# A four-layer graph attention stack: token blocks moved by DMA and transposed on VectorE in layers 0 and 2, and exp read straight from the score bank

## The chip, the cores and the metric

The kernel runs on one core of a Trainium2 chip. A core has TensorE (PE; its weight loads are shown apart as PEld), VectorE (DVE), ScalarE (ACT), GpSimd (POOL) and SyncE (SP), each with its own queue of instructions that it works through in order. SP issues most of the DMAs. The metric is the device time of the whole program in microseconds, as a median over runs.

## The reference, cut to what matters

The input `x` has 128 graphs of 64 nodes with 512 features, `adj` says which nodes are joined. Four layers follow each other, all in fp32:

```python
for layer in 0, 1, 2, 3:
    h = relu(layernorm(x))            # per node, over 512 features
    x = x + attention_layer(h, adj)

# layers 0 and 2: 4 heads of 64
q, k, v = h @ Wq, h @ Wk, h @ Wv      # 512 -> 256 each
s = where(adj, q k^T / 8, -max)
out = softmax(s) v @ Wo + bo
# layer 1: 8 heads, a second layernorm with gamma and beta ahead of q, k, v
# layer 3: 8 heads, a map, cosine neighbours, a softmax, a graph convolution, relu
```

The nodes of all graphs make 8192 rows ("tokens"). TensorE contracts over partitions, so the projections need `h` with features on partitions, `hT`, while the layernorm works with tokens on partitions. Something has to transpose every layer's normalised tokens.

## The kernel before, in words

The 8192 tokens are worked in 16 steps of 512 per layer; `(l, s)` names step `s` of layer `l`. A step's tokens are one tile `xin` of 128 partitions by 4 blocks of 512 features. Two such tiles exist. One step goes through these stages, each written as a Python generator:

- `loads` (line 470) brings `xin` in by two DMAs on SP, from the input or from the layer before, which was stored in DRAM.
- `layernorms` (496) takes the statistics on VectorE, the power of -1/2 on POOL, and normalises on ScalarE, in place in `xin`.
- `transposes` (554) makes `hT` (two buffers). In layers 0 and 2, and in the first two steps of layers 1 and 3, TensorE transposes 16 blocks of 128x128 into PSUM banks `ptr`, four to a group (570), and ScalarE copies each group of four into `hT` (574). In steps 2 to 15 of layers 1 and 3 `turned_tokens` (510) does it without TensorE: ScalarE and POOL copy sixteen 32x512 pieces of `xin` into a buffer `t` so that the 32x32 blocks stand in their places (534, 531), and VectorE's transpose, which turns each 32x32 block in itself, finishes (544).
- `sums_of_b` (356) makes on POOL the four differences that a seven-product (Winograd) scheme needs, in a buffer `t` (three exist).
- `projections` (729) runs the products, all at line 613 in PSUM banks `mA`, `mB` and `mC`. Results come out by ScalarE copies (630, 650) and VectorE adds (643, 654).
- `front` (1158) makes the scores (930) into `sc`, and `softmax_parts` (934) masks them on VectorE (941), takes the row maximum (947), subtracts it into an SBUF tile `E` (949), which gives the score bank back, and takes exp on ScalarE (952). Row sums (959), a reciprocal (963) and a product on POOL (965) follow. The bank `sc` is a single one, and the products of attention and values, `po` (1097), use the same.
- `turns` and `transposed` (967) transpose the attention with ScalarE copies (974) and VectorE (979). `attention` (1075) forms `po`, the output projection (613 again) and its adds to the residual `xres`, on POOL (1024, 1045) and VectorE (643). `store` (1058) writes the result by SP (1065). `residuals` (1009) loads `xres` by SP (1020), `masks` (983) loads `adj` (988).

The order of instructions on each engine is not written out by hand. A small planner, `Order` (93), takes the generators with priorities. Each `yield` names an engine and an assumed duration, such as `act(0.6)`; a wait is a `yield` of an event. The planner runs the generators against each other on these assumed durations and emits the instructions in the order that results. On the chip each engine follows that order, with semaphores for the data. Buffers come from rings: `Ring.new` (165) waits in the plan for the buffer's last user. The ring `qk` (three buffers of 128x2048 fp32) holds the projected queries and keys.

Of the kernel before, what the change touches and what calls it, by code (L numbers as in the profile page):

```python
# [10 lines left out]
AF = mybir.ActivationFunctionType  # L11
ALU = mybir.AluOpType
AX = mybir.AxisListType

P = 128
D = 512
N = 64
TB = 4
NC = D // P
# [184 lines left out]
def pe(us):  # L204
    return ("pe", us, 0.25)
# [6 lines left out]
def dve(us):  # L212
    return ("dve", us, 0.1)


def act(us):
    return ("act", us, 0.1)
# [11 lines left out]
def gnn_stack(ctx: ExitStack, tc: tile.TileContext, a: dict, out: bass.AP):  # L229
    nc = tc.nc  # L230
    x_d = a["x"]
    NG = x_d.shape[0] // (P * TB)
    od = Order()

    def ring(tag, n, shape, dtype=F32, space=None):
        kw = {} if space is None else {"space": space}
        p = ctx.enter_context(tc.tile_pool(name=tag, bufs=n, **kw))
        return Ring(od, p, n, shape, dtype, tag)
# [12 lines left out]
    r_h = ring("h", 2, [P, NC, TB * P])  # L251
    r_t = bank("t", 3, [P, NC, 2, H])
    r_qk = ring("qk", 3, [P, NC, TB * P])
# [15 lines left out]
    x_done = {}  # L269
# [86 lines left out]
    def sums_of_b(B, T, vector=False):  # L356

        n = T.shape[2]
        for o, i0, i1 in ((T[:, 0], B(0, 1), B(0, 0)), (T[:, 1], B(1, 1), T[:, 0]),
                          (T[:, 2], B(1, 1), B(0, 1)), (T[:, 3], B(1, 0), T[:, 1])):  # L360
            if vector:
                yield dve(0.9)
                nc.vector.tensor_tensor(o, i0, i1, ALU.subtract)  # L363
            else:
                yield pool(1.42)
                nc.gpsimd.tensor_tensor(o, i0, i1, ALU.subtract)  # L366
# [70 lines left out]
    def scales(v):  # L437

        mv = small.tile([P, 2, 2], F32, tag="mv", name="mv")
        for t in range(2):  # L440
            st = small.tile([P, 6], F32, tag="st", name="st")
            yield dve(0.68)
            nc.vector.bn_stats(st, v[:, t, :])  # L443
            yield dve(0.17)
            nc.vector.bn_aggr(mv[:, t, :], st)
        rs = small.tile([P, 3, 2], F32, tag="rs", name="rs")
        yield dve(0.25)
        nc.vector.tensor_scalar_add(rs[:, 1, :], mv[:, :, 1], LN_EPS)  # L448
        yield pool(0.75)
        nc.gpsimd.tensor_tensor(rs[:, 0, :], rs[:, 1, :], mhalf[:, :2], ALU.pow)  # L450
        yield dve(0.45)
        nc.vector.scalar_tensor_tensor(rs[:, 2, :], mv[:, :, 0], -1.0, rs[:, 0, :],  # L452
                                       ALU.mult, ALU.mult)
        return rs

    def normalize(v, rs, func):
        for t in range(2):
            yield act(0.81)
            nc.scalar.activation(v[:, t, :], v[:, t, :], func, bias=rs[:, 2, t:t + 1],  # L459
                                 scale=rs[:, 0, t:t + 1])  # L460

    hT, hB, h_ready, h_done, t_done = {}, {}, {}, {}, {}

    def quarters(v):

        return lambda j, k: v[:, 2 * j:2 * j + 2, k * H:(k + 1) * H]

    loaded, l_ready = {}, {}

    def loads(steps):  # L470
        for l, s in steps:
# [22 lines left out]
    normed, n_ready = {}, {}  # L494

    def layernorms(steps, half):

        for l, s in steps:
            yield l_ready[l, s, half]
            whole, xe = loaded.pop((l, s, half))  # L500
            x = whole[:, 2 * half:2 * half + 2, :]
            rs = yield from scales(x)
            yield from normalize(x, rs, AF.Relu)
            if l == 1:
                rs = yield from scales(x)
                yield from normalize(x, rs, AF.Identity)
            normed[l, s] = whole, xe
            n_ready[l, s, half].set()

    def turned_tokens(l, s):  # L510
# [40 lines left out]
        h_ready[l, s].set()  # L551
        return h

    def transposes(steps):

        for l, s in steps:
            if (l, s) in [(1, 2), (1, 3), (1, 4), (1, 5), (1, 6), (1, 7), (1, 8), (1, 9), (1, 10), (1, 11), (1, 12), (1, 13), (1, 14), (1, 15), (3, 2), (3, 3), (3, 4), (3, 5), (3, 6), (3, 7), (3, 8), (3, 9), (3, 10), (3, 11), (3, 12), (3, 13), (3, 14), (3, 15)]:
                h = yield from turned_tokens(l, s)
            else:
                h, h_done[l, s] = yield from r_h.new("hT")  # L560
                hT[l, s] = h
            for half in range(0 if (l, s) in [(1, 2), (1, 3), (1, 4), (1, 5), (1, 6), (1, 7), (1, 8), (1, 9), (1, 10), (1, 11), (1, 12), (1, 13), (1, 14), (1, 15), (3, 2), (3, 3), (3, 4), (3, 5), (3, 6), (3, 7), (3, 8), (3, 9), (3, 10), (3, 11), (3, 12), (3, 13), (3, 14), (3, 15)] else 2):
                yield n_ready[l, s, half]
                x, xe = normed[l, s]
                for t in range(2):
                    b = 2 * half + t
                    pt, pe_ = yield from r_tr.new("ptr")
                    for c in range(NC):
                        yield pe(0.115)
                        nc.tensor.transpose(pt[:, c, :], x[:, b, c * P:(c + 1) * P], ident)  # L570
                    if b == TB - 1:
                        xe.set()
                    yield act(0.6)
                    nc.scalar.copy(h[:, :, b * P:(b + 1) * P], pt)
                    pe_.set()
                if (l, s, half) == (0, 0, 0):
                    yield from has_h(l, s, h)
            if (l, s) != (0, 0) and (l, s) not in [(1, 2), (1, 3), (1, 4), (1, 5), (1, 6), (1, 7), (1, 8), (1, 9), (1, 10), (1, 11), (1, 12), (1, 13), (1, 14), (1, 15), (3, 2), (3, 3), (3, 4), (3, 5), (3, 6), (3, 7), (3, 8), (3, 9), (3, 10), (3, 11), (3, 12), (3, 13), (3, 14), (3, 15)]:
                yield from has_h(l, s, h)
            yield from sums_of_b(quarters(h), hB[l, s][1], (l, s) == (0, 0))  # L580
            hB[l, s][2].set()
            if (l, s) == (0, 0):
                first_t.set()

    def has_h(l, s, h):
        T, t_done[l, s] = yield from r_t.new("T")
        hB[l, s] = (quarters(h), T, od.event())
        h_ready[l, s].set()
# [138 lines left out]
    st, p_ready, s_ready, p_used, o_used, turn = {}, {}, {}, {}, [], []  # L727
# [203 lines left out]
                                         lT[r, c, k], rT[r, c, k], start=True, stop=True)  # L931
        return S, e

    def softmax_parts(S, se, E, mask, neg, masked):

        m = mask.rearrange("p b k -> p (b k)")
        n = m.shape[1]
        sv = S.rearrange("p a (c m) -> p (a c) m", m=n)
        shape = [P, 1024 // n, n]
        yield dve(1.5)  # L940
        nc.vector.copy_predicated(sv, m[:, None, :].to_broadcast(shape),
                                  negs[:, neg:neg + 1, None].to_broadcast(shape))
        masked.set()
        S3 = S.rearrange("p a (i k) -> p (a i) k", k=N)
        mx = soft.tile([P, 16], F32, tag="mx", name="mx")
        yield dve(1.2)
        nc.vector.tensor_reduce(mx, S3, AX.X, ALU.max)
        yield dve(1.2)
        nc.vector.tensor_tensor(E, S3, mx[:, :, None].to_broadcast([P, 16, N]), ALU.subtract)  # L949
        se.set()  # L950
        yield act(1.06)
        nc.scalar.activation(E, E, AF.Exp, scale=0.125)  # L952
        sm = soft.tile([P, 2, 16], F32, tag="sm", name="sm")
        yield from row_sums(sm[:, 0, :], E)
        return sm

    def row_sums(o, E):
        yield dve(1.2)
        nc.vector.tensor_reduce(o, E, AX.X, ALU.add)  # L959
# [230 lines left out]

    def softmax(l, z, u, S, se, m, masked):
        E = z["e", u][0]
        sm = yield from softmax_parts(S, se, E, m, (0, 1, 0, 2)[l], masked)
        z["sm", u] = sm
        if l < 3:
            yield from divide(E, sm[:, 0, :])
            z["e_ready", u].set()
        z["exp", u].set()
# [73 lines left out]

    steps = [(l, s) for l in range(4) for s in range(NG)]
    for k in steps:
        for e in (p_ready, s_ready, p_used, h_ready, x_done):
            e[k] = od.event()
        for half in range(2):
            l_ready[(*k, half)], n_ready[(*k, half)] = od.event(), od.event()
    with tc.manual_schedule():
        od.spawn(weights(), 4)  # L1280
        od.spawn(loads(steps), 4)
        for half in range(2):
            od.spawn(layernorms(steps, half), 4)
        od.spawn(transposes(steps), 3)
        od.spawn(projections([k for k in steps if k[0] < 3]), 5)
        od.spawn(fronts(steps), 1)
        od.spawn(turns(steps), 1)
        od.spawn(attentions(steps), 2)
        od.run()
# [45 lines left out]
```

## Time and profile before

| What | Value |
|---|---|
| Median of 3 runs | 2790.13 us (2788.91 to 2795.86) |
| Profiled execution, its own time | 2791.22 us |
| Its span, first to last instruction | 2789.2 us |
| Mean granted TensorE clock | 0.993 |
| Busy share PE, PEld, DVE, ACT, POOL | 98%, 85%, 68%, 67%, 58% |
| TensorE transposes `ptr` (line 570) | 576 records |
| DMA | 238.51 MB in 160430 packets |

A page row gives the line, engine, operation, output and inputs, shapes and count, then the busy time in us and the mean ns of one, and last the idle time of that engine just before, with what ended it. A fp32 product appears as two records of line 613, a transpose as one. In the chain of waits the columns are who waited, for whom, the total in us, how often, and the longest. "SPq" is SP's queue of DMA issues.

### The profile page before, as it was taken

To read this page: it belongs to the slowest core of one execution; us is meant where nothing else is said; L and a number is where in the kernel's file an instruction comes from. 1 tells how busy PE (TensorE), PEld (TensorE's weight loads), DVE (VectorE), ACT (ScalarE), POOL (GpSimd) and SP (SyncE) were. 2 spreads that over 40 slices of the span, in tenths; PEclk is the share of its full clock that TensorE was granted. 3 is DMA by queue.
4 is the path that set the end of the run, shared out by engine and by line. 5 is a ranking of instruction groups with operands and counts; after the bars stand their busy time and mean duration, and the time that the engine had idled before them with its cause. 6 is when DMAs were issued, how large, how long until landed. Compare 5 with 4: busy or idle time off the path is not lost.

```text
span 2789.2 us, 63654 instructions
## 1 busy us (share of the span) xinstructions
PE 2723.9 (98%) x26728; PEld 2362.1 (85%) x26728; DVE 1896.2 (68%) x2780; ACT 1872.4 (67%) x3149; POOL 1608.2 (58%) x1242
## 2 busy tenths in 40 slices
PE   8999999999999999999999999999999999999997
PEld 7888888888888888888888888878888888888876
DVE  6766767677767667766657666746777667776656
ACT  5756756688777777776656656657566776677644
POOL 5667667645435445446656576676665656555543
PEclk9999999999999999999999999999999999999998
DMA  4333333212112111112322242332422233223221
GB/s 157 108 107 109 108 116 114 96 63 77 47 62 77 47 61 64 61 47 97 122 93 92 93 138 93 108 104 78 111 64 63 71 93 86 64 63 84 73 63 47
DMA packets 160430, 238.51 MB, mean 86 GB/s; under 512 B 23952, under 2 KB 69008, under 8 KB 160144
## 3 DMA queue, kind: packets, MB, share of 16 engines
q1 hardware_dynamic: 145632, 219.98, 25.4%
q10 hardware_dynamic: 14512, 14.47, 1.6%
q8 instruction: 210, 3.44, 0.5%
q14 instruction: 76, 0.62, 0.1%
HBM read 166.77 MB, written 67.63 MB: 84 GB/s over the span
## 4 chain that ended last, share of the span: by engine, by line
PE 91%; DVE 4%; POOL 2%; ACT 1%; issue 1%; DMA 1%; POOLq 0%; SPq 0%; ACTq 0%; DVEq 0%
PE mA L613 46%; PE mC L613 23%; PE mB L613 12%; PE sc L930 5%; PE po L1097 2%; PE ptr L570 2%; PE po L1242 1%; PE mmn L872 1%; POOL xres L1045 1%; POOL xres L1024 1%; ACT F L974 1%; DVE xres L643 1%; DVE E L949 0%; DVE t L363 0%; POOL E L965 0%
## 5 line engine op out<-in xcount | busy, mean ns | idle before, releaser
L974 ACT COPY F<-E 32x512 f32<-32x512 f32 x768 | 472.5, 615 | 41.0 <-POOL E L965 26.3
L1045 POOL TENSOR_TENSOR xres<-xres,u 128x512 f32<-128x512 f32 x192 | 259.9, 1361 | 296.3 <-ACT u L1040 236.1
L1024 POOL TENSOR_TENSOR xres<-xres,u 128x512 f32<-128x512 f32 x192 | 260.8, 1380 | 23.0 <-DMA xres<-x 17.0
L366 POOL TENSOR_TENSOR t<-hT 128x512 f32<-128x512 f32 x126 | 181.4, 1440 | 145.7 <-DVE hT L544 89.0
L459 ACT ACTIVATE xin<-xin,rs 128x512 f32<-128x512 f32 x320 | 247.8, 810 | 19.4 <-DVE rs L452 15.6
L630 ACT COPY v<-mA 128x256 f32<-128x256 f32 (+1 forms) x192 | 92.0, 479 | 218.5 <-PE mA L613 205.5
L534 ACT COPY t<-xin 32x512 f32<-32x512 f32 x364 | 224.1, 616 | 6.4
L450 POOL TENSOR_TENSOR rs<-rs,mhalf 128x2 f32<-128x2 f32 x160 | 115.9, 726 | 192.0 <-DVE rs L448 168.7
L443 DVE BATCH_NORM_STATS2 st<-xin 128x6 f32<-128x512 f32 x320 | 214.9, 672 | 15.8 <-DMA xin<-in_x 7.7
L613 PE MATMUL mA<-w_vo,t 128*128 128x128 f32 (+1 forms) x1152 | 204.5, 312 | 1.1 <-ACT u L1040 1.1
L613 PE MATMUL mA<-t,w_qk 128*128 128x256 f32 x768 | 185.9, 381 | 1.5 <-DVE t L363 1.5
L965 POOL TENSOR_TENSOR E<-E,sm 128x1024 f32<-128x1024 f32 x64 | 127.8, 1997 | 100.6 <-DVE sm L963 87.3
L613 PE MATMUL mA<-t,w_q 128*128 128x256 f32 x744 | 179.2, 383 | 0.0
L613 PEld LDWEIGHTS mA<-w_vo,t 128*128 128x128 f32 x1152 | 166.2, 191 | 14.6 <-ACT u L1040 4.3
L613 PE MATMUL mA<-t,w_k 128*128 128x256 f32 x744 | 177.3, 381 | 0.0
L366 POOL TENSOR_TENSOR t<-hT,t 128x512 f32<-128x512 f32 x126 | 168.3, 1336 | 7.7 <-DVE hT L544 4.2
L959 DVE TENSOR_REDUCE sm<-E 128x16 f32<-128x1024 f32 x128 | 154.9, 1210 | 12.8 <-ACT E L952 12.1
L613 PEld LDWEIGHTS mA<-t,w_qk 128*128 128x128 f32 x768 | 144.4, 192 | 20.3 <-DVE t L363 1.7
L613 PEld LDWEIGHTS mA<-t,w_q 128*128 128x128 f32 x744 | 140.5, 191 | 20.8 <-issue 1.2
L613 PEld LDWEIGHTS mA<-t,w_k 128*128 128x128 f32 x744 | 140.3, 190 | 19.4
L979 DVE STREAM_TRANSPOSE pt<-F 128x1024 f32<-128x1024 f32 x96 | 118.7, 1236 | 49.8 <-ACT F L974 49.6
L1040 ACT COPY u<-mA 128x512 f32<-128x512 f32 x144 | 84.4, 586 | 97.7 <-PE mA L613 88.8
(217 smaller groups left out, 6908.9 us busy)
## 6 DMA issues: line engine op xcount, KB each, us to landing
x<-xres SPq DMA_DIRECT2D x96, 512.0 KB
xin<-x SPq DMA_DIRECT2D x96, 512.0 KB
xres<-x SPq DMA_DIRECT2D x64, 512.0 KB
xres<-in_x SPq DMA_DIRECT2D x32, 512.0 KB
u<-rs SPq DMA_DIRECT2D x128, 128.0 KB
xres<-x SPq DMA_DIRECT2D x64, 256.0 KB
out<-xres SPq DMA_DIRECT2D x64, 256.0 KB
xin<-in_x SPq DMA_DIRECT2D x30, 512.0 KB
```

Source lines behind the costliest of these rows:

```text
L366: nc.gpsimd.tensor_tensor(o, i0, i1, ALU.subtract)
L443: nc.vector.bn_stats(st, v[:, t, :])
L459: nc.scalar.activation(v[:, t, :], v[:, t, :], func, bias=rs[:, 2, t:t + 1], scale=rs[:, 0, t:t + 1])
L534: nc.scalar.copy(o, v)
L613: nc.tensor.matmul(o, l, r, start=(first and m == 0 and k == 0), stop=(k == KC - 1), skip_group_check=True)
L930: nc.tensor.matmul(S[g * N:(g + 1) * N, par, col], lT[r, c, k], rT[r, c, k], start=True, stop=True)
L959: nc.vector.tensor_reduce(o, E, AX.X, ALU.add)
L965: nc.gpsimd.tensor_mul(E, E, sm[:, :, None].to_broadcast([P, 16, N]))
L974: nc.scalar.copy(F[g * N + 32 * k:g * N + 32 * (k + 1), :, 32 * i:32 * (i + 1)], E[g * N + 32 * i:g * N + 32 * (i + 1), :, 32 * k:32 * (k ...
L979: nc.vector.transpose(o, F)
L1024: nc.gpsimd.tensor_add(xr[:, t, :], xr[:, t, :], bo[l])
L1045: nc.gpsimd.tensor_add(v, v, both(u))
```

## The change

In steps 2 to 15 of layers 0 and 2 the tokens are no longer transposed on TensorE. A new stream `moves` issues sixteen DMAs on SP for each step, from SBUF to SBUF. Each takes 32 partitions of the normalised `xin` and writes, in pieces of 32 numbers, 32 partitions of a buffer `F` from the ring `qk`, so that the 32x32 blocks stand in their places. `by_vector` then turns the blocks with two VectorE transposes into `hT`. TensorE's transposes and ScalarE's copies out of `ptr` go away for these 28 steps. `xin` is given back when the DMAs have read it, and a step's moves wait, in the plan, until the `F` before has been turned.

In all steps of layers 0 and 2 the softmax no longer subtracts the maximum on VectorE. It multiplies the maximum by -1/8, and ScalarE takes exp from the score bank in sixteen instructions of 64 columns, each with its own row maximum as bias, into `E`. The score bank is given back after the last of them.

```diff
+    def moves(steps):
+        fe = None
+        for l, s in steps:
+            for half in range(2):
+                yield n_ready[l, s, half]
+            if fe:
+                yield fe
+            x, xe = normed.pop((l, s))
+            F, fe = yield from r_qk.new("F")
+            Fv = F.rearrange("p c n -> p (c n)").rearrange("p (a i f) -> p a i f", i=4, f=32)
+            xv = x.rearrange("p b (c k f) -> p (b c) k f", c=NC, k=4)
+            for k in range(4):
+                for i in range(4):
+                    yield ("sp", 0.7, 4.0)
+                    nc.sync.dma_start(Fv[32 * k:32 * (k + 1), :, i], xv[32 * i:32 * (i + 1), :, k])
+            xe.set()
+            before, fe = fe, od.event()
+            moved[l, s] = F, before, fe
+            f_ready[l, s].set()
+
+    def by_vector(l, s):
+        yield f_ready[l, s]
+        F, fe, taken = moved.pop((l, s))
+        h, h_done[l, s] = yield from r_h.new("hT")
+        hT[l, s] = h
+        F = F.rearrange("p c n -> p (c n)").rearrange("p (b c n) -> p b c n", b=TB, c=NC)
+        for b in range(0, TB, 2):
+            yield dve(1.25)
+            nc.vector.transpose(h.rearrange("p c (b n) -> p b c n", b=TB)[:, b:b + 2], F[:, b:b + 2])
+        fe.set()
+        taken.set()
+        return h
...
     def transposes(steps):
         for l, s in steps:
-            if (l, s) in [(1, 2), ... (3, 15)]:
+            if (l, s) in by_dma:                      # steps 2 to 15 of layers 0 and 2
+                h = yield from by_vector(l, s)
+            elif (l, s) in turned:                    # steps 2 to 15 of layers 1 and 3
                 h = yield from turned_tokens(l, s)
...
-        yield dve(1.2)
-        nc.vector.tensor_tensor(E, S3, mx[:, :, None].to_broadcast([P, 16, N]), ALU.subtract)
-        se.set()
-        yield act(1.06)
-        nc.scalar.activation(E, E, AF.Exp, scale=0.125)
+        if narrow:                                    # layers 0 and 2
+            yield dve(0.1)
+            nc.vector.tensor_scalar(mx, mx, -0.125, None, ALU.mult)
+            for i in range(16):
+                yield act(0.21)
+                nc.scalar.activation(E[:, i, :], S3[:, i, :], AF.Exp, bias=mx[:, i:i + 1], scale=0.125)
+            se.set()
+        else:
+            yield dve(1.2)
+            nc.vector.tensor_tensor(E, S3, mx[:, :, None].to_broadcast([P, 16, N]), ALU.subtract)
+            se.set()
+            yield act(1.06)
+            nc.scalar.activation(E, E, AF.Exp, scale=0.125)
...
+        od.spawn(moves(by_dma), 3)
         od.spawn(transposes(steps), 3)
```

More of the change, by code (lines that the diff above doesn't have):

```diff
@@ L466, in quarters @@
         return lambda j, k: v[:, 2 * j:2 * j + 2, k * H:(k + 1) * H]
-    loaded, l_ready = {}, {}
+    loaded, l_ready, moved, f_ready = {}, {}, {}, {}
+    by_dma = [(0, 2), (0, 3), (0, 4), (0, 5), (0, 6), (0, 7), (0, 8), (0, 9), (0, 10), (0, 11), (0, 12), (0, 13), (0, 14), (0, 15), (2, 2), (2, 3), (2, 4), (2, 5), (2, 6), (2, 7), (2, 8), (2, 9), (2, 10), (2, 11), (2, 12), (2, 13), (2, 14), (2, 15)]
+    turned = [(1, 2), (1, 3), (1, 4), (1, 5), (1, 6), (1, 7), (1, 8), (1, 9), (1, 10), (1, 11), (1, 12), (1, 13), (1, 14), (1, 15), (3, 2), (3, 3), (3, 4), (3, 5), (3, 6), (3, 7), (3, 8), (3, 9), (3, 10), (3, 11), (3, 12), (3, 13), (3, 14), (3, 15)]
     def loads(steps):
@@ L552, in turned_tokens @@
         return h
+    def moves(steps):
[29 more added lines that the diff above has]
+        return h
     def transposes(steps):
         for l, s in steps:
-            if (l, s) in [(1, 2), (1, 3), (1, 4), (1, 5), (1, 6), (1, 7), (1, 8), (1, 9), (1, 10), (1, 11), (1, 12), (1, 13), (1, 14), (1, 15), (3, 2), (3, 3), (3, 4), (3, 5), (3, 6), (3, 7), (3, 8), (3, 9), (3, 10), (3, 11), (3, 12), (3, 13), (3, 14), (3, 15)]:
+            if (l, s) in by_dma:
+                h = yield from by_vector(l, s)
+            elif (l, s) in turned:
                 h = yield from turned_tokens(l, s)
@@ L561, in transposes @@
                 hT[l, s] = h
-            for half in range(0 if (l, s) in [(1, 2), (1, 3), (1, 4), (1, 5), (1, 6), (1, 7), (1, 8), (1, 9), (1, 10), (1, 11), (1, 12), (1, 13), (1, 14), (1, 15), (3, 2), (3, 3), (3, 4), (3, 5), (3, 6), (3, 7), (3, 8), (3, 9), (3, 10), (3, 11), (3, 12), (3, 13), (3, 14), (3, 15)] else 2):
+            for half in range(0 if (l, s) in turned + by_dma else 2):
                 yield n_ready[l, s, half]
@@ L577, in transposes @@
                     yield from has_h(l, s, h)
-            if (l, s) != (0, 0) and (l, s) not in [(1, 2), (1, 3), (1, 4), (1, 5), (1, 6), (1, 7), (1, 8), (1, 9), (1, 10), (1, 11), (1, 12), (1, 13), (1, 14), (1, 15), (3, 2), (3, 3), (3, 4), (3, 5), (3, 6), (3, 7), (3, 8), (3, 9), (3, 10), (3, 11), (3, 12), (3, 13), (3, 14), (3, 15)]:
+            if (l, s) != (0, 0) and (l, s) not in turned:
                 yield from has_h(l, s, h)
@@ L932, in scores, with softmax_parts @@
         return S, e
-    def softmax_parts(S, se, E, mask, neg, masked):
+    def softmax_parts(S, se, E, mask, neg, masked, narrow=False):
         m = mask.rearrange("p b k -> p (b k)")
@@ L1192, in softmax @@
         E = z["e", u][0]
-        sm = yield from softmax_parts(S, se, E, m, (0, 1, 0, 2)[l], masked)
+        sm = yield from softmax_parts(S, se, E, m, (0, 1, 0, 2)[l], masked, l in (0, 2))
         z["sm", u] = sm
@@ L1274, in gnn_stack @@
     for k in steps:
-        for e in (p_ready, s_ready, p_used, h_ready, x_done):
+        for e in (p_ready, s_ready, p_used, h_ready, f_ready, x_done):
             e[k] = od.event()
```

## The prediction

> **What bounds the kernel now.** I read the page first: busy time by engine, and the chain of work that ended last.
>
> ```profile
> PE 2723.9 (98%) x26728; PEld 2362.1 (85%) x26728; DVE 1896.2 (68%) x2780; ACT 1872.4 (67%) x3149; POOL 1608.2 (58%) x1242
> PE 91%; DVE 4%; POOL 2%; ACT 1%; issue 1%; DMA 1%; POOLq 0%; SPq 0%; ACTq 0%; DVEq 0%
> ```
>
> TensorE is busy for 98% of the span and carries 91% of the chain; nothing else is near. An average hides stages, so I then took busy time by stretches: two inside layers 0 and 2, which the change touches, and one in layer 1. The columns are the stretch, its length, then busy microseconds of PE, weight loads, DVE, ACT and POOL, the granted clock, DMA share and GB/s.
>
> ```profile
> 200.00:340.00 140.00, 138.60 (x1340) 124.25 (x1339) 99.66 (x158) 90.52 (x156) 94.49 (x73) 1.00 0.36 115
> 560.00:900.00 340.00, 339.85 (x3084) 294.06 (x3083) 237.41 (x352) 266.77 (x412) 162.07 (x136) 1.00 0.19 63
> 1560.00:1700.00 140.00, 135.57 (x1356) 120.17 (x1355) 89.52 (x141) 85.35 (x145) 91.33 (x71) 0.99 0.34 115
> ```
>
> Layers 0 and 2 are TensorE-bound too, with a little idle time. Over 60 to 480 us, PE is idle 420 - 410.7 = 9.3 us, over 1420 to 1840 us 13.7 us: 23 us in some 29 steps, 0.8 us a step. A step (one `sc` group to the next, 264.04 to 292.80) lasts 28.8 us. So what leaves TensorE's queue here is gained, unless something else becomes late by more. Next, who makes PE wait in 60 to 480 us (the chain of waits, PE), and what SP's queue waits for:
>
> ```profile
> PE mC L613 <- DVE xres L643: 3.6, 2, 1.8
> PE mB L613 <- DVE xres L643: 2.6, 2, 1.3
> PE po L1097 <- DVE E L949: 2.4, 3, 1.0
> ```
>
> ```profile
> SPq L486 <- PE ptr L570: 201.9, 14, 24.6
> SPq L1065 <- DVE xres L643: 144.6, 15, 29.6
> SPq L1020 <- DMA x<-xres: 37.0, 25, 4.0
> ```
>
> PE's few waits are for residual adds on DVE, and for the score bank that L949 gives back. SP is idle most of the time: its loads stand ready and wait for `xin`, given back by the transposes, and its stores for the last residual add. Input arrives long before its use, which gives a longer way to `hT` room.
>
> **What a transpose group costs.** The timeline, PE's weight loads around one group:
>
> ```profile
> 243.17 0.41 PEld L613 LDWEIGHTS mA<-w_vo,t 128*128 128x128 f32 x2
> ...
> 243.60 0.57 PEld L570 LDWEIGHTS ptr<-ident,xin 128*128 128x128 f32 x4
> ...
> 244.14 0.30 PEld L613 LDWEIGHTS mA<-w_vo,t 128*128 128x128 f32 x2
> ```
>
> From the group's first load to the next product's is 244.14 - 243.60 = 0.54 us, the same at 248.79, 250.52, 257.44 and 272.32. There is no bubble before it: two loads of `mA` take 0.43 us here and elsewhere.
>
> **What the Trainium skill says.** "DMA: Bandwidth & Descriptors", Specifications, says that transfers under 512 B fall below line rate because they are read, modified and written. The trace agrees: its packet records give 97 ns for 2 KB packets (21 B/ns), 12.6 ns for the 4096 of 128 B (10 B/ns), half the rate but far from a fixed cost of a large packet. "ScalarE: Activation LUTs", What ACT_TABLE_LOAD costs, prices an ACTIVATE with a per-partition bias at 280 ns + 0.833 ns an element, neighbours overlapping by 93 ns; L634 (256 elements) took 471 ns where this gives 493, so the trace is a little below it.
>
> **The change, by parts.** Rows used (groups by shape):
>
> ```profile
> L574 ACT COPY hT<-ptr 128x512 f32<-128x512 f32 x144 | 84.4, 588 | 14.7 <-PE ptr L570 13.1 <-issue 1.0
> L949 DVE TENSOR_TENSOR E<-sc,mx 128x1024 f32<-128x1024 f32 x96 | 117.0, 1219 | 1.8
> L952 ACT ACTIVATE E<-E 128x1024 f32<-128x1024 f32 x96 | 101.5, 1057 | 9.4 <-DVE E L949 8.9
> L979 DVE STREAM_TRANSPOSE pt<-F 128x1024 f32<-128x1024 f32 x96 | 118.7, 1236 | 49.8 <-ACT F L974 49.6
> L634 ACT ACTIVATE kT<-mA,vecs 128x256 f32<-128x256 f32 x96 | 40.3, 471 | 27.6 <-PE mA L613 26.7
> ```
>
> *Off TensorE:* 28 steps x 4 groups x 0.54 = 60.5 us. The chain's share of `ptr` (2.0%, 56 us over 576) would give 448 x 0.097 = 43 us, its busy time (90.5 us over 576) 70 us. I take 60: pace in the queue is what TensorE gets back. Nothing is added to TensorE.
>
> *ScalarE, a step:* four copies go, 4 x 0.588 = 2.35, and one exp, 1.06. Sixteen exps of 64 columns come. From L634, one takes 471 - 192 x 0.836 = 310 ns (the slope from copies of 256 and 512 columns, 372 and 586), and follows its neighbour after about 0.21 (pairs of L459, 0.81 each, take 1.52). So +3.5, up to 16 x 0.31 = 5.0. Net +0.05 to +1.6 us. ScalarE stands at 90.5/140, 18.6 us of a step of 28.7; with 18.6 to 20.2 in a step of 26.5, 70 to 76%. Hidden under TensorE.
>
> *VectorE, a step:* L949 goes (1.22), a 128x16 multiply comes (about 0.16, as L448), and two transposes of 1.24. Net +1.4. From 20.4 to 21.8 us in 26.5: 82%. Hidden, but this is the engine whose in-order queue holds the residual adds that PE waits for; without cover it would cost 28 x 1.4 = 39 us. POOL keeps its work, 19.4 us, 73% of the shorter step.
>
> *The score bank:* it is held by the sixteen exps rather than until the subtract. That is +0.16 + 3.5 - 1.22 = +2.4 us, with interleaved copies perhaps 4. There is one bank, which `po` needs. Now the subtract ended at 243.15 and `po` followed at 258.61: 15 us spare. In the built order, in the steady part, some 15 us of products stand between `sc` and `po` again. Cost nothing; without that cover 32 x 2.4 = 77 us.
>
> *SP and DMA, a step:* sixteen moves of 64 KB in 128 B pieces. Present issues take 0.36 to 0.63 us (L1020 to L1154), so 5.8 to 10 us on SP over the 2.9 us there; no present issue has 512 pieces. Below, a move could cost 0.36; above, the 1.4 us each that two of L1020 once took (2.86 at 325.95). I take 0.6. The engines' time is 8192 packets x 12.6 ns / 16 = 6.5 us on 0.36 x 28.7 = 10.3: 63% of a step, no bound.
>
> *Order:* in the built order some twelve moves stand before a step's store and four behind it, and behind these the next loads of `xres` and `xin`. The loads of `xin` wait until the moves land; each move waits for the DMA eight before it. The store waits for the last residual add, with the moves behind it queued on SP. Then `xin` must land before VectorE's statistics, ahead of the next residual adds on its queue. I sum this way from the last add: POOL 1.3, stores 0.7, four moves 2.4, landing 3, `xres` 0.4, `xin` issue 0.5 and landing 4, 12 to 13 us. Both landings are estimates: a store kept SP waiting 37.0/25 = 1.5 us more, while the first load of all, at the start, took 7.1 us in the chain. Statistics stand some two thirds of a step later, about 18 us. Slack 5 us, or 2 with a landing of 7. So it is hidden, but this is the thinnest cover.
>
> *Sum:* -60.5, and I let PE's idle time of 0.8 us a step grow by half as VectorE fills: 28 x 0.4 = +11. Net -49.5. The profiled execution took 2791.2 (span 2789.2), 1 us over the median of 2790.1; from the median, **2740**.
>
> **Rivals.**
>
> *Half is eaten:* VectorE at 82% in program order delays residual adds and bank releases more than I allow: 0.7 to 1.8 us a step, 20 to 52 us, 2750 to 2782, centre 2765. For: PE's present waits are of this kind. Against: in layer 1 VectorE is 70% busy and ScalarE 78%, and PE idles 0.15 us in 340.
>
> *SP sets the step (slower):* if a move holds SP for 1.9 us (piece generation at 512 pieces, or waiting for the DMA eight before it to land), SP needs 16 x 1.9 + 2.9 = 33.3 us, 4.6 over the present step: 28 x 4.6 = +129, near 2920; at 1.75, 2855. It bites from (26.5 - 2.9)/16 = 1.47 us and loses from (28.7 - 2.9)/16 = 1.6. Against: the longest ordinary issue is 0.63.
>
> *The score bank* could replace the wait removed: were the spare of 15 us gone, +77 - 60 gives 2807. Speaks for it only that `po` already waited for L949 three times, at most 1.0 us.
>
> **How the numbers follow.** Gain kept (2724 to 2748): 0.58. Half eaten: 0.25, and with it a remainder near no change, 0.04. SP: 0.10. Bank: 0.03. The range is 2722 to 2784, leaving some 0.16 outside, mostly above; the likeliest case's own range is 2724 to 2748. About 0.3%, 8 us, is what a measurement can tell from no change: faster 0.83, same 0.04, slower 0.13.
>
> **What would show it.** Right: PE's busy time down by about 60 us, `ptr` at 128 records; sixteen exps some 0.2 us apart; moves issued in under 0.8 us; PE idle in layers 0 and 2 about 34 us over those 28 steps. Wrong: PE waits for `hT` or `t` behind F, VectorE waits at its F transposes or statistics for DMA, SP's issues well over 1 us, or `po` waits for the exps.

## The result: 2751.9 us, 39 us faster

| | before | after |
|---|---|---|
| Median | 2791.27 us (2788.91 to 2795.86) | 2751.89 us (2749.39 to 2755.36) |
| Ratio to before, 95% interval | | 0.9855 [0.9839, 0.9871] |
| Profiled execution, its span | 2791.2, 2789.2 us | 2751.8, 2750.0 us |
| Mean granted TensorE clock | 0.993 | 0.991 |

The forecast was 2740 us with a range of 2722 to 2784. Direction and range hold. Of the net 49.5 us that the sum gave, 39 arrived, which is outside the likeliest case's own range (2724 to 2748) and at the edge of "half is eaten".

The busy times by engine and the chain that ended last, after:

```profile
PE 2678.9 (97%) x26280; PEld 2320.6 (84%) x26280; DVE 1956.6 (71%) x2836; ACT 1889.6 (69%) x3517; POOL 1615.5 (59%) x1242
PE 91%; DVE 4%; ACT 2%; DMA 1%; SPq 1%; POOL 1%; issue 1%; POOLq 0%; ACTq 0%; DVEq 0%
```

TensorE is still the bound. Its busy time fell by 45.0 us and its idle time rose from 65.3 to 71.1 us (span less busy): -45.0 + 5.8 = -39.2, the whole difference. The three engines beside it rose by 60, 17 and 7 us, and the chain gives the three together 7%, as before.

SP's moves, by the tile `F` (shortest, median and longest in ns), and two groups by shape:

```profile
L571 SPq DMA_DIRECT2D F<-xin x448: 585/631/2797, 46.1 to 1731.7; - x150
```

```profile
L586 DVE STREAM_TRANSPOSE hT<-F 128x1024 f32<-128x1024 f32 x56 | 67.0, 1223 | 0.7 <-DMA F<-xin 0.6
L992 ACT ACTIVATE E<-sc,mx 128x64 f32<-128x64 f32 x512 | 122.0, 352 | 21.6 <-DVE mx L989 21.3
```

A move holds SP for 0.63 us at the median (0.6 was taken). VectorE waited for a move once, 0.6 us: the moves land in time. A narrow exp takes 352 ns by itself (310 estimated), and ten in a row took 2.19 us, so one follows its neighbour after 0.20 (0.21 taken). `ptr` fell from 576 records to 128. SP's queue now waits for the normalised `xin` rather than for the transposes (chain of waits, SP, 60 to 460 us, two of its lines):

```profile
SPq L571 <- ACT xin L459: 88.6, 10, 12.9
...
SPq L1035 <- DMA w_k<-in_Wk: 5.9, 1, 5.9
```

The same stretches as before, with two more (columns as in the prediction: stretch, length, busy PE, weight loads, DVE, ACT, POOL, clock, DMA share, GB/s). First before, the two that were not shown:

```profile
60.00:200.00 140.00, 136.51 (x1357) 121.83 (x1348) 101.97 (x157) 92.10 (x157) 92.76 (x71) 1.00 0.30 97
460.00:540.00 80.00, 78.09 (x692) 68.08 (x691) 58.07 (x96) 51.15 (x83) 57.05 (x45) 1.00 0.41 137
```

After:

```profile
60.00:200.00 140.00, 121.08 (x1163) 105.79 (x1161) 105.42 (x162) 91.13 (x206) 96.11 (x76) 0.95 0.56 141
460.00:540.00 80.00, 74.13 (x725) 64.85 (x724) 61.72 (x93) 53.89 (x98) 59.50 (x47) 0.97 0.38 130
200.00:340.00 140.00, 139.28 (x1358) 124.41 (x1359) 111.89 (x168) 91.45 (x209) 89.77 (x69) 0.99 0.61 154
1560.00:1700.00 140.00, 139.51 (x1368) 124.72 (x1367) 116.38 (x177) 99.19 (x233) 101.42 (x78) 1.00 0.59 153
```

The steady parts are better than hoped: PE idles 0.7 us in 140 where it idled 1.4 (layer 0), and 0.5 where it idled 4.4 (layer 2). The loss stands in two other places. At the start of layer 0, PE idles 18.9 us against 3.5 and its clock falls to 0.95; at the border to layer 1 it idles 5.9 against 1.9, with a clock of 0.97. The chain of waits of PE, after, names four stalls in these places:

```profile
PE mC L652 <- ACT v L669: 5.8, 2, 5.1
PE po L1144 <- DVE mv L445: 5.4, 1, 5.4
PE mA L652 <- DVE hT L586: 5.2, 1, 5.2
PE mA L652 <- ACT u L1087: 4.5, 1, 4.5
```

By the trace they stand near 62 to 67 us (`hT`), 156 to 160 (`u`), 195 to 200 (`v`) and 531 to 537 (`mv`). The first can be followed on SP's timeline:

```profile
52.95 3.48 SPq L571 DMA_DIRECT2D F<-xin  x5
62.43 0.35 SPq L1035 DMA_DIRECT2D adj<-in_adj  x1
62.82 1.60 SPq L571 DMA_DIRECT2D F<-xin  x2
```

The load of `adj` (L1035) stood between two moves of step 2 and waited the 5.9 us of the line above for the landing of a weight load (`w_k`). The two moves behind it went out at 62.8, VectorE turned the tile at 65.95 and PE went on at 67.34. The next two are copies on ScalarE that stood behind copies of the attention into `F` (L1021), which themselves waited for POOL. At the border (`mv`) the event named is only the last one: the transposed attention that this `po` reads was ready at 536.60, and eight such copies on ScalarE, from 529.82 to 535.32, stood before it.

What the sixteen exps leave free is small. One step of layer 2, from the timelines of PE, its weight loads and ScalarE:

```profile
1608.22 1.16 PE L969 MATMUL sc<-qk 64*64 64x64 f32 x64
1617.92 0.97 PEld L652 LDWEIGHTS mA<-w_vo,t 128*128 128x128 f32 x8 [0.22 <-ACT v L669]
1618.20 0.57 ACT L992 ACTIVATE E<-sc,mx 128x64 f32<-128x64 f32 x2
1619.46 1.16 PE L1144 MATMUL po<-pt,v 64*64 64x64 f32 x64
```

The last exp ends at 1618.77 and gives the score bank back; `po`, which uses the bank, begins 0.7 us later. The weight load before it waits for a copy of `v` that stands behind ten of the exps on ScalarE. There are 10 such waits in 1380 to 1830 us, 2.7 us in all.

### The profile page after: what moved, and what is told of

Read it like the earlier page. It is cut to its first block, busy times and chain, and to the rows that moved or that the text cites. A ratio compares the mean times of both kernels' runs of the same rounds, so it can differ in the third digit from the quotient of the medians.

```text
span 2750.0 us, 63860 instructions
## 1 busy us (share of the span) xinstructions
PE 2678.9 (97%) x26280; PEld 2320.6 (84%) x26280; DVE 1956.6 (71%) x2836; ACT 1889.6 (69%) x3517; POOL 1615.5 (59%) x1242
## 4 chain that ended last, share of the span: by engine, by line
PE 91%; DVE 4%; ACT 2%; DMA 1%; SPq 1%; POOL 1%; issue 1%; POOLq 0%; ACTq 0%; DVEq 0%
PE mA L652 46%; PE mC L652 23%; PE mB L652 12%; PE sc L969 5%; PE po L1144 2%; PE po L1289 1%; ACT F L1021 1%; SPq L571 1%; PE mmn L911 1%; DVE mx L986 0%; PE ptr L609 0%; DMA F<-xin 0%; ACT E L992 0%; DVE st L443 0%; DVE sc L980 0%
## 5 line engine op out<-in xcount | busy, mean ns | idle before, releaser
L1021 ACT COPY F<-E 32x512 f32<-32x512 f32 x768 | 472.6, 615 | 46.1 <-POOL E L1012 28.7
L366 POOL TENSOR_TENSOR t<-hT,t 128x512 f32<-128x512 f32 x126 | 175.5, 1393 | 8.0 <-DVE hT L546 4.2
L652 PEld LDWEIGHTS mA<-t,w_k 128*128 128x128 f32 x744 | 140.2, 190 | 19.4
```

The source lines that it names most:

```text
L652: nc.tensor.matmul(o, l, r, start=(first and m == 0 and k == 0), stop=(k == KC - 1), skip_group_check=True)
L1021: nc.scalar.copy(F[g * N + 32 * k:g * N + 32 * (k + 1), :, 32 * i:32 * (i + 1)], E[g * N + 32 * i:g * N + 32 * (i + 1), :, 32 * k:32 * (k ...
```

## Experiments

Two theories went in. **Transition**: the steady step gains what was summed, and the rest is lost at layer 0's start and its border. **Half eaten**: VectorE, at 80 and 83% in the stretches of layers 0 and 2 above, delays others all along. A third came up with the first runs: that the order of instructions, and not their work, decides.

### One part alone

The moves with the softmax of before:

```diff
-        sm = yield from softmax_parts(S, se, E, m, (0, 1, 0, 2)[l], masked, l in (0, 2))
+        sm = yield from softmax_parts(S, se, E, m, (0, 1, 0, 2)[l], masked)
```

> The moves in layers 0 and 2, the softmax as before. Theory A (the moves carry the gain, the exps cost nothing and give nothing): the same as the changed kernel, 2745 to 2758. Theory B (the sixteen exps make the softmax late in layer 0, which is where the gain is lost): faster than the changed kernel by 10 to 20 us, 2732 to 2742, with PE's idle time in the first 200 us back near that of before. Theory C (the exps relieve VectorE, which the moves load): slower than the changed kernel, 2760 or more.

Measured: 2806.5 us, 1.0061 [1.0046, 1.0076]. The 28 steps of transposes have left TensorE, and the kernel is slower than before. The new softmax alone:

```diff
+    by_dma = [k for k in by_dma if False]            # no step moves by DMA
```

> The sixteen exps in layers 0 and 2, tokens transposed on TensorE everywhere as before. Theory A: no change from before, within 5 us of 2791. Theory B: slower than before by 10 to 20 us, the loss in layer 0. Theory C: the same as before or a few us faster, since VectorE has 1.1 us a step less to do.

Measured: 2785.5 us, 0.9984 [0.9977, 0.9991]. So the two parts are worth +17 and -4 us alone and -39 together. In the moves alone PE waits 18 times for a copy of `u`, 43.8 us in all. One of the long steps of its layer 0, with the lines of POOL, ScalarE and PE from their timelines:

```profile
375.85 1.90 POOL L1012 TENSOR_TENSOR E<-E,sm 128x1024 f32<-128x1024 f32 x1 [9.77 <-DMA F<-xin]
...
377.79 2.50 ACT L1021 COPY F<-E 32x512 f32<-32x512 f32 x4 [2.65 <-POOL E L1012]
380.31 0.59 ACT L1087 COPY u<-mA 128x512 f32<-128x512 f32 x1
...
380.95 2.07 PE L652 MATMUL mA<-w_vo,t 128*128 128x256 f32 x4 [3.98 <-ACT u L1087]
```

The last bracket is PE's idle time. The attention copies wait for POOL's product of the softmax, the copy of `u` stands behind four of them in ScalarE's queue, and PE stands behind `u`. No engine is full: in 340 to 480 ScalarE is busy for 73.8 of 140 us and VectorE for 103.4. The releaser named for POOL is only the last event that the profile has; VectorE's reciprocal for this product ended at 375.71, by its timeline.

### One layer alone

```diff
+    by_dma = [k for k in by_dma if k[0] == 2]        # and the softmax: l == 2; or 0 in both
```

> Both parts in layer 2 alone. If the traces' reading holds (layer 2 gains some 40 us, layer 0 nothing net), 2750 to 2755: the whole gain with half of the change. If the gain is spread evenly over both layers and the rest is a matter of where work is counted, 2770 to 2774.

> Both parts in layer 0 alone. If layer 0's gain is eaten by the stalls of the first 200 us and of the border to layer 1, 2786 to 2794, no change. If the gain is even over both layers, 2770 to 2774.

Measured: layer 2 alone 2753.96 us, 0.9872 [0.9857, 0.9887]; layer 0 alone 2790.0 us, 1.0 [0.9991, 1.0009]. Layer 2 gives 35.6 us, layer 0 nothing. Layer 0 alone shows the same two weak places as the changed kernel (PE busy 120.99 of 140 in 60 to 200 and 74.28 of 80 in 460 to 540).

### The start of layer 0

```diff
+    by_dma = [k for k in by_dma if k[0] == 2 or k[1] >= 7]
```

> The changed kernel, but in layer 0 the moves begin with step 7, so that TensorE transposes steps 2 to 6 while the weights come in. If the loss of layer 0 comes from its first 200 us (moves beside weight loads and half-filled buffers), this keeps the gain of nine of fourteen steps there and of layer 2: 2728 to 2742. If the loss is in the order at the border to layer 1 or is spread over layer 0, 2750 to 2758.

Measured: 2768.1 us, 0.9923 [0.9908, 0.9937], 16 us above the changed kernel and above both forecasts. Five steps are back on TensorE, some 11 of the 16 us (5 x 2.1, worked out below). PE is busy for 138.70 us in 60 to 200, so the early stalls are gone; but for only 127.56 in 200 to 340, where the moves now begin, and for 68.26 of 80 in 460 to 540, at a clock of 0.91. The cost of a start went along with it and the border got worse: an early start that collides with weight loads is one stall of several, not the whole cause.

### More work on VectorE

One more maximum of 1.22 us in every softmax of layers 0 and 2, whose output is not used:

```diff
+            spare = soft.tile([P, 16], F32, tag="spare", name="spare")
+            yield dve(1.2)
+            nc.vector.tensor_reduce(spare, S3, AX.X, ALU.max)
```

> The changed kernel with one more VectorE reduction of the score bank (1.22 us, its result unused) in each softmax of layers 0 and 2, so that VectorE has as much to do as with the moves and the old subtract. If VectorE's time is what makes the moves lose without the exps: 2780 to 2810, near the moves alone (2806). If the loss comes from the order that the planner happens to find there, or from ScalarE's side, VectorE's extra time stays hidden: 2750 to 2762.

Measured: 2751.0 us, 0.9866 [0.985, 0.9883]. The stretch of layer 2:

```profile
1560.00:1700.00 140.00, 140.00 (x1387) 125.63 (x1386) 123.63 (x182) 98.38 (x224) 102.55 (x79) 1.00 0.58 156
```

VectorE is busy for 123.63 of 140 us, 88%, and PE does not idle at all. "Half eaten" falls, at least as a load of the engine: VectorE fuller than the change made it costs nothing here. The extra instruction also made another order, in which the early loss of layer 0 stands in part later (PE idles 8.5 us in 60 to 200 and 10.2 in 200 to 340), so the run shows that this load fits under one good order, not that it does under every one.

### The order, or the work

The softmax's instructions carry assumed durations, so swapping them lets the planner make another order on every engine. First two kernels with nothing changed but one such number, in the moves alone (1.06 to 1.16) and in the changed kernel:

```diff
-                yield act(0.21)
+                yield act(0.24)
```

> The moves alone again, with the planner's assumed duration of the old exp at 1.16 instead of 1.06 us; the chip does the same work in another order. If the moves alone lose because of a load, the time stays at 2800 to 2812. If it is the order, it moves by more than 10 us, likely downwards: 2760 to 2795.

> The changed kernel with the planner's assumed duration of a narrow exp at 0.24 instead of 0.21 us: the same work in another order. If the order matters little with VectorE relieved, 2748 to 2758. If the order decides, it is off by more than 10 us to either side.

Measured: 2814.2 us, 1.0092 [1.0077, 1.0108], and 2761.1 us, 0.9901 [0.9886, 0.9916]. The first lies above both of its forecasts, the second between them. Orders of one kind differ by some 8 to 13 us (8 and 9 by the times, 9 and 13 by the ratios to before); that does not bridge the 55 between the moves alone and the changed kernel. Then the two were crossed. Old work in the new order:

```diff
             yield dve(0.1)
-            nc.vector.tensor_scalar(mx, mx, -0.125, None, ALU.mult)
+            nc.vector.tensor_tensor(E, S3, mx[:, :, None].to_broadcast([P, 16, N]), ALU.subtract)
             for i in range(16):
                 yield act(0.21)
-                nc.scalar.activation(E[:, i, :], S3[:, i, :], AF.Exp, bias=mx[:, i:i + 1], scale=0.125)
+            nc.scalar.activation(E, E, AF.Exp, scale=0.125)
             se.set()
```

> The order of instructions on TensorE, VectorE, GpSimd and SP is exactly that of the changed kernel, but the work in the softmax of layers 0 and 2 is the old one: the subtract of 1.22 us stands where the small multiply stood, and one exp of 1.06 us where the sixteenth narrow exp stood. Theory 'order': the moves without the new exp lost because the planner, which assumed 2.3 us for maximum to exp, put the users of the softmax too early in the in-order queues; with the sixteen exps it assumed 3.5 us and made an order with room. Then this kernel stays near the changed one, 2745 to 2765 us. Theory 'work': it is the subtract and the wide exp themselves (VectorE held 1.2 us longer in the softmax, the ScalarE queue behind it) that stall TensorE; then it lands with the moves alone, 2795 to 2815.

and new work in the old order:

```diff
             yield dve(1.2)
-            nc.vector.tensor_tensor(E, S3, mx[:, :, None].to_broadcast([P, 16, N]), ALU.subtract)
-            se.set()
-            yield act(1.06)
-            nc.scalar.activation(E, E, AF.Exp, scale=0.125)
+            nc.vector.tensor_scalar(mx, mx, -0.125, None, ALU.mult)
+            for i in range(16):
+                nc.scalar.activation(E[:, i, :], S3[:, i, :], AF.Exp, bias=mx[:, i:i + 1], scale=0.125)
+            se.set()
+            yield act(1.06)
```

> The mirror image: order on TensorE, VectorE, GpSimd and SP exactly that of the moves alone, which took 2806 us, but with the multiply and the sixteen narrow exps in place of the subtract and the wide exp, all sixteen emitted in one place. Theory 'order': still slow, 2800 to 2825, some us worse than 2806 since the exps take 1.2 us longer than subtract and wide exp did. Theory 'work': near the changed kernel, 2750 to 2770.

Measured: 2748.4 us, 0.9849 [0.9835, 0.9864], and 2924.8 us, 1.0479 [1.0461, 1.0497]. The first settles it: with subtract and wide exp back, but in the order that the sixteen made (by the traces the same on TensorE, GpSimd and SP, and on VectorE but for the exchanged instruction), the whole gain is there. The narrow exps in themselves give nothing; the interval overlaps that of the changed kernel. In the order of the moves alone they lose another 118 us, 100 us above the slower of the two forecasts. This mirror is not exact, since ScalarE's order is not that of the moves alone: the sixteen stand in one block, 30 times of 32 one or two ScalarE instructions before the place of the wide exp, and the changed kernel has copies of `v` between them. PE waits 31.8 us for `v`, which stands behind them, and 20.2 us for the bank that they hold.

What the good order looks like: `sc` and `po` on PE's timeline, old work in the new order, layer 2,

```profile
1580.68 1.16 PE L969 MATMUL sc<-qk 64*64 64x64 f32 x64
...
1591.62 1.16 PE L1144 MATMUL po<-pt,v 64*64 64x64 f32 x64
...
1607.64 1.16 PE L969 MATMUL sc<-qk 64*64 64x64 f32 x64
```

and the moves alone, layer 0:

```profile
340.65 1.16 PE L969 MATMUL sc<-qk 64*64 64x64 f32 x64
...
365.83 1.16 PE L969 MATMUL sc<-qk 64*64 64x64 f32 x64
...
372.25 1.16 PE L1144 MATMUL po<-pt,v 64*64 64x64 f32 x64
...
391.04 1.16 PE L1144 MATMUL po<-pt,v 64*64 64x64 f32 x64
...
403.83 1.16 PE L969 MATMUL sc<-qk 64*64 64x64 f32 x64 [1.51 <-ACT qk L669]
```

In the first, one step is like the next: 26.96 us here and again to the next `sc` at 1634.60. In the second, short and long steps take turns, 25.2 and 38.0 us here, with two `po` between two `sc`. ScalarE's queue shows what follows. In the first the eight attention copies are done before the copies of `u` begin (timeline of ScalarE):

```profile
1570.42 1.88 ACT L1021 COPY F<-E 32x512 f32<-32x512 f32 x3 [0.71 <-POOL E L1012]
...
1576.95 0.61 ACT L1021 COPY F<-E 32x512 f32<-32x512 f32 x1
1580.35 0.59 ACT L1087 COPY u<-mA 128x512 f32<-128x512 f32 x1 [0.28 <-PE mA L652]
```

In the second they stand in between, at 377.79 and 380.31 as shown above. What in the plan makes the good order was tried once more, with the longer softmax alone:

```diff
-            yield act(1.06)
+            yield act(2.3)                            # layers 0 and 2, old work, moves as in the change
```

> The moves with the old softmax work (subtract, then one wide exp; the bank given back after the subtract), and one constant changed: in layers 0 and 2 the planner assumes 2.3 us for the wide exp in place of 1.06, so 3.5 us from the maximum to the end of exp, as with the sixteen. The order that helps has two parts that are still mixed: the longer softmax, and the bank given back after it in the plan (with places between the sixteen where other ScalarE work may stand). If the longer softmax alone makes the good order, this lands at 2745 to 2770 us. If it takes the later release of the bank in the plan, or the places between, it stays with the moves alone, 2795 to 2820.

Measured: 2813.3 us, 1.0084 [1.0067, 1.0102]. The longer assumed softmax is not it. The later release of the bank in the plan, the places between the sixteen, and a chance of how the planner's priorities fall remain; these three were not told apart.

What goes with the time is how often two `po` follow each other. Counted in layers 0 and 2 of the traces, without each layer's last step, that is 8, 9 and 6 times in the moves alone (2806 us), in their second order (2814) and with the longer assumed exp (2813), twice in the changed kernel with 0.24 (2761), and once in the changed kernel, with the second maximum, and with the old work in the new order (2748 to 2752). The pair by itself is not the whole of it: without the moves it stands four times before and never with the new softmax, and these two are only 4 us apart. That it causes the loss is thus argued, not shown. In the changed kernel the one pair is in layer 0, and the stall for `u` named above stands in it, the one for `v` in the step after it (PE's timeline):

```profile
151.44 1.16 PE L1144 MATMUL po<-pt,v 64*64 64x64 f32 x64
...
160.37 2.08 PE L652 MATMUL mA<-w_vo,t 128*128 128x256 f32 x4 [4.50 <-ACT u L1087]
...
169.78 1.16 PE L1144 MATMUL po<-pt,v 64*64 64x64 f32 x64
```

With the late start the pair comes at 233.77 and 251.84 us, with a stall of 4.50 for `u`; with the second maximum at 210.26 and 226.97, with one of 3.10. So a part of what layer 0 lost at its start is the order too.

### The cover on SP

Each move as two of 16 partitions, issued in the same place, so all else keeps its order:

```diff
-                    nc.sync.dma_start(Fv[32 * k:32 * (k + 1), :, i], xv[32 * i:32 * (i + 1), :, k])
+                    for c in (0, 16):
+                        nc.sync.dma_start(Fv[32 * k + c:32 * k + c + 16, :, i],
+                                          xv[32 * i + c:32 * i + c + 16, :, k])
```

> The changed kernel with each move split in two of 16 partitions (256 pieces of 128 B each) issued back to back, so 32 DMAs a step in place of 16, same bytes, same pieces, same order of all else. The prediction held SP to be the thinnest cover: it bites from 23.6 us of moves in a step. If an issue costs 0.63 us whatever its pieces, SP is held 32 x 0.63 + 2.9 = 23 us of a step of 27, the landing of xin comes 2.4 us or more later than the 5 us of slack allows in some steps, and the kernel takes 2765 to 2800. If an issue of half the pieces takes about 0.35 us, SP is held 14 us as before and it stays at 2748 to 2758.

Measured: 2927.95 us, 1.0491 [1.0474, 1.0509], 176 us above the changed kernel and worse than either theory said. An issue of 256 pieces costs as much as one of 512, and VectorE now waits for the moves (by the tile `F`, then the chain of waits of VectorE; the lines of the code stand one or two further down here):

```profile
L572 SPq DMA_DIRECT2D F<-xin x896: 585/607/2619, 45.8 to 1910.4; - x180
```

```profile
DVE hT L588 <- DMA F<-xin: 122.0, 23, 11.8
```

The moves of a step hold SP for 32 x 0.607 = 19.4 us in place of 16 x 0.631 = 10.1. With the 2.9 us of before that is 22.3, still below a step of 27. SP even stands idle before a step's moves, in layer 2 for 7.6 us from 1583.8. So it is not SP's sum that bites; what fits is the loop that the prediction priced: moves, landing, next `xin`, statistics, next moves. It grew by 9.3 us, PE's idle time by 131/28 = 4.7 us a step, and the kernel, whose clock is lower too, by 176/28 = 6.3. What was hidden is thus some 3 to 5 us (an estimate, since a new stall also shifts others), and the prediction had put the slack at 5 or 2.

## Why the prediction was right, and where it was not

- **"28 steps x 4 groups x 0.54 = 60.5 us"** holds for a regular step. The new softmax without the moves runs without stalls: `sc` follows `sc` in 58.15 us for two steps (1605.68 to 1663.83), 29.08 each. Without transposes it is 26.96, with the old work in the new order and in layer 0 of the changed kernel (320.21 to 347.18). The difference is 2.12 us, 0.53 a group. In layer 2 of the changed kernel a step takes 27.25: 0.29 more, which fits the waits for `v` behind the exps (10 in layer 2, none with the old work in the new order).
- **"PE's idle time grows by half as VectorE fills", +11 us,** is the step that failed, in place and in size. In the steady steps idle time did not grow, it shrank: with layer 2 alone changed PE is busy for 435.0 of the 440 us from 1380 to 1820, where it was 430.1. These 4.9 us and 14 x 2.12 = 29.7 make 34.6 of the 35.6 measured. In layer 0 the same 29.7 us were lost again at the start and the border: 15.4 us more idle time and 0.05 x 121 = 6 of slower clock in 60 to 200, 4.0 and 0.03 x 74 = 2 in 460 to 540, some 27 us in all; as its steady part idles 3.7 us less too, some 6 us of layer 0 stay open. The sum had priced a steady step 28 times and no transition between kinds of steps. The lower clock also makes the busy time a poor witness: it fell by 45 us, not by 28 x 2.12 = 59; the clock explains 8 of the difference, the waits for `v` in layer 2, in which PE counts as busy, some 3 to 4, and the rest is less than the busy times of before and of the new softmax alone differ (2723.9 and 2730.4 us) with as many instructions on TensorE.
- **ScalarE's and VectorE's loads hidden**: right but for the 0.29 us a step above, and for VectorE shown beyond the change by the second maximum.
- **The score bank's longer hold hidden by 15 us**: hidden, but not by 15. In the changed kernel's regular steps the last exp ends 0.4 to 0.7 us before `po`, as shown with the result. The hold itself was sized well: the bank is given back 10.55 us after `sc` began, and 6.45 after it with the old work in the same order, 4.1 longer ("perhaps 4"). The cover had been read from one roomy step. Before, it differed from step to step: after the `sc` at 290.54 the subtract ended at 296.86 and `po` followed at 297.19. With the sixteen in one block in the other order the hold cost 20 us of PE's waits.
- **SP "the thinnest cover"**: right in that the change just clears it, and in its size, 3 to 5 us; the bank's was thinner.
- **"Half is eaten"** ended near the measured time by another way; its reason, VectorE in program order, is refuted as a matter of load; what ate the gain stands at layer 0's start and border. **"SP sets the step"** had a rule that was wrong: with two half moves of 0.607 us for each, SP's sum stays below the 1.47 us a move from which it should bite, and the loop bit all the same.
- Three slips of its working decide nothing. The `sc` after 264.04 is at 290.54 us, not 292.80, so that step is 26.5 us; layer 0's steps before run from 19.3 to 40.5 and average 29.3, where 28.8 was used. At 1.75 us a move the rival's sum gives 2852, not 2855, and 28 x 1.8 is 50, not 52.
- What the prediction took for granted, that the built order carries the gain, was its largest risk. It priced the softmax's edit as engine work hidden under TensorE. Its effect was the order, worth 55 us: without it the moves lose 17, and the same sum would have been wrong. In this the forecast had luck.

## What to carry to other kernels

When a planner sets the order from assumed durations, an edit is its work and its new order; cross the two (the old work at the new places) before crediting the work. Price the first and last steps of a new kind apart from the steady ones: here layer 0 lost there what its steady steps gained, and layer 2 did not. Read a cover from several steps, not from one. An issue of 256 pieces held its queue as long as one of 512: cut a move finer only where the loop through that queue has room.

## What was not expected of the hardware

- **Stalls of TensorE cost twice.** The kernel with halved moves runs the very TensorE instructions of the changed kernel in the same order. Its PE busy time is 2725.2 us against 2678.9, +46 us beside +131 of idle time, at a mean clock of 0.971 against 0.991 and of 0.89 in 60 to 340 us. The Trainium skill, "TensorE: Matmul & The Clock Gate", Part 1: The HAM clock gate, says that the clock is set by how busy the array has lately been; the traces agree, since the low clocks stand in stretches with stalls, and the halved kernel's stretch from 960 to 1380 us, busy for 419.85 of 420, has 1.00.
- **An issue of half the pieces is not cheaper**: 0.607 us for 256 pieces of 128 B, 0.631 for 512, both at the median.
- **Small pieces stayed cheap at scale**: over 233472 packet records of 128 B the mean is 13.8 ns (12.6 for the 4096 of before), with the DMA engines busy for some 0.6 of the time in the steady stretches.
- **A DMA issue can wait for a stranger**: SP's `adj` load waited 5.9 us for a weight load that ScalarE's queue had issued, though neither needs the other's data. In the trace both signal semaphore 100, one of eight that the program's DMAs use, and the load waits on it: the wait comes from how the program shares out semaphores.
